# Interleaving the normalisation of a triangle product with output units that do not need it, in a two-layer kernel

## The chip, the core and the metric

One core of one Trainium2 chip runs the whole kernel. The engines named below are TensorE (PE; PEld is its weight load), VectorE (DVE), ScalarE (ACT), GpSimd (POOL) and the queue of SyncE (SP), which here only issues transfers. The metric is the device time of one execution in microseconds; the time of a kernel is the median of its runs.

## The reference, cut to what matters

The input x is 512 x 512 positions of 64 channels. Layer 0 normalises it by groups, then works on the normalised value `x`:

```python
xn = _ln(x, norm_w, norm_b)                       # over the 64 channels
left  = (xn @ left_w  + left_b)  * mask * sigmoid(xn @ lgate_w + lgate_b)
right = (xn @ right_w + right_b) * mask * sigmoid(xn @ rgate_w + rgate_b)
out_gate = sigmoid(xn @ ogate_w + ogate_b)
out = einsum('bkjd,bkid->bijd', left, right)      # the triangle product
out = (_ln(out, onorm_w, onorm_b) @ out_w + out_b) * out_gate
x1 = x + out
...
x2 = x1 + spectral(group_norm(x1))                # layer 1: 12 x 12 Fourier modes
```

The mask is 1 where both the row and the column of a position are set. At most 256 of the 512 rows are set in this case, so the product has to be formed for 256 x 256 positions only. A row that is not set has a product of zero: its `_ln(...) @ out_w + out_b` is the same 64 numbers for every column.

## The kernel before, in words

The function `compact` does the work. Rows are ranked so that the set rows come first. Four stages follow one another: (1) statistics of x for the group norm, (2) left and right for the set rows and columns, (3) the triangle product, written to DRAM as `tri_d` one channel at a time, (4) the stage that the change touches, followed by the last one, (5), which adds the inverse transform to x1 and writes the output.

Stage 4 has a hand-written order (`tc.manual_schedule()`): a loop over steps s (L1193) emits, for each step, one instruction group after another, and every engine runs its own instructions in that order. Eight steps (`SIZE`) make a unit. There are two kinds of unit.

* **Product units** (`first` = 8 of them, L920, the first 64 steps). A unit is 32 columns of the product. A step loads 512 positions of `tri_d` (`load_product`, L1022, on the SP queue, six steps ahead of use), multiplies them by a joint weight `both` = [centring matrix | output weight] (`centered`, L1048, matmul at L1058: eight matmuls over 64 rows each), squares one half of the result on ACT (L1078) and copies the other half to SBUF (L1079). Every two steps DVE sums the squares into `totals` (L1083). Once per unit ACT takes the square root (`root`, L1089) and DVE the reciprocal (L1263), into `factors`. DVE multiplies by the factors (L1271), POOL adds the bias row (L1278), and SP writes the result to `u_d` in DRAM.
* **Gate units** (32 of them, `units`, L922: column block `jc` of 16, `half` 0 for set rows and 1 for the others). A unit is 32 columns by 256 rows of x, gathered by POOL's indirect transfers (`load`, L1091). A step transposes 512 positions (`transpose`, L1030; PE at L1038, ACT's copy at L1040), multiplies them by `center_x` (`times`, L1045, tile c_ps) and, 12 steps later, by `gate_x` (tile w_ps). ACT squares c_ps (L1076), DVE sums (L1083), and root and reciprocal give `rs_n`. DVE multiplies w_ps by it (L1274) and adds the gate's bias (L1280), ACT takes the sigmoid (L1221), POOL multiplies by u (`gated`, L1109: a row of `u_d`, fetched by `load_u` at L1097, for half 0, the bias row for half 1) and adds to x (`added`, L1113). DVE takes the statistics of the sum for layer 1 (L1168, 32 instructions a unit), PE transforms it along the rows (`transform`, L1140), `save` (L1146) keeps the modes of both halves of one column block together, and SP stores x1.

`LEAD` = 13 steps lie between the transpose of a step and its multiplication by the factors. `scratch`, which holds totals, factors, the bias rows and sums of the statistics, lies in PSUM; x, u, z, the squares and the statistics lie in SBUF. The helper `rsqrt_steps` (L197 to L215) is an inverse square root of nine DVE instructions (L204 to L214); its tiles v, w, h and y lie in SBUF. Stage 2 uses it for its own norm, three instructions at a time from a list `todo`; stage 4 does not.

Of the kernel before, what the change touches and what calls it, by code (L numbers as in the profile page):

```python
# [17 lines left out]
P = 128  # L18
N = 512
# [27 lines left out]
def conv_preact_kernel(ctx: ExitStack, tc: tile.TileContext, t: dict):  # L47
# [149 lines left out]
    def rsqrt_steps(pool, total, scale, eps, shape, y=None):  # L197

        v, w, h, out = (pool.tile(shape, F32, name="rq_" + k) for k in ("v", "w", "h", "out"))
# [421 lines left out]
    def compact(fc):  # L621
# [4 lines left out]
        modes_d = dram.tile([N, M2, C], F32, name="modes_d")  # L626
# [204 lines left out]
        with tc.tile_pool(name="tri", bufs=1) as trp:  # L831
# [88 lines left out]
            first = K * 2 // 64  # L920

            units = [(jc, half) for jc in range(NJ) for half in ((1, 0) if jc < NJ - 1 else (0, 1))]  # L922
            total_g = (first + len(units)) * SIZE
            with tc.manual_schedule(), tc.tile_pool(name="late", bufs=1) as lp:
# [23 lines left out]
                def columns(h, pool):  # L948

                    q = P if h < 3 else P - JC  # L950
                    by = modes_t.rearrange("p (m k) c -> p m (k c)", k=2)
                    ps = pool.tile([P, 4, P], F32, name="t_ps").rearrange("p i k -> p (i k)")[:, : MODES * M2]
                    ps = ps.rearrange("p (m n) -> p m n", m=MODES)
                    for m in range(MODES):
                        nc.tensor.matmul(ps[:, m, :], by[:q, m, :], col_basis[:q, h, :], start=h < 3 or m == 0, stop=h < 3)
                    if h < 3:
                        nc.vector.tensor_add(sums, sums, ps)
                    return ps

                def fetch(h):  # L960

                    q = P if h < 3 else P - JC
                    (nc.scalar if h == 3 else nc.sync).dma_start(modes_t[:q], modes_d[h * P : h * P + q])
# [26 lines left out]
                with tc.tile_pool(name="np_x", bufs=LEAD + 2) as tp, tc.tile_pool(name="np_q", bufs=2) as sqp, tc.tile_pool(  # L990
                    name="np_s", bufs=3
                ) as small, tc.tile_pool(name="oz", bufs=4) as zp, tc.tile_pool(
                    name="o1", bufs=1
                ) as s1, tc.tile_pool(name="np_n", bufs=1, space=PSUM) as ps_n, tc.tile_pool(name="opf", bufs=1, space=PSUM) as ps_f, ExitStack() as products:
# [4 lines left out]
                    both = lp.tile([P, P], F32, name="both")  # L999
                    for h in range(2):  # L1000
                        hs = slice(h * C, (h + 1) * C)
                        nc.vector.tensor_copy(both[hs, :C], center[hs, hs])
                        nc.vector.tensor_copy(both[hs, C:], weights["out"][hs, hs])
# [15 lines left out]
                    def x_of(k):  # L1019
                        return place(order[k % RING])  # L1020
# [9 lines left out]
                    def transpose(s):  # L1030
                        k, n = divmod(s, SIZE)
                        if k < first:
                            return
                        flat = x_of(k - first).rearrange("p n c -> p (n c)")
# [4 lines left out]
                        xts[s] = tp.tile([P, 4, P], F32, name="xt_c")  # L1039
# [8 lines left out]
                    def centered(s):  # L1048
                        if s >= first * SIZE:
                            return times(ps_c, "c_ps", s, center_x)  # L1050

                        ps = ps_y.tile([P, 2, 4, P], F32, name="y_ps")
                        q, e = divmod(s, 2)
                        of = products_t[q % 4][:, e * N : (e + 1) * N].rearrange("p (i k) -> p i k", i=4)
                        for i in range(4):
                            for h in range(2):
                                hs = slice(h * C, (h + 1) * C)
                                nc.tensor.matmul(ps[:, h, i, :], of[hs, i, :], both[hs], start=True, stop=True)  # L1058
# [4 lines left out]
                    def raw(s):  # L1063
                        return xts[s].rearrange("p h (i c) -> p (h i) c", c=C).rearrange("p (h i) c -> p h i c", h=2)
# [5 lines left out]
                    def squared(s, cps):  # L1070
# [4 lines left out]
                        if s >= first * SIZE:  # L1075
                            nc.scalar.activation(sq, cps, AF.Square)  # L1076
                        else:
# [56 lines left out]
                    def transform(k, r):  # L1134
                        jc, half = units[k]
                        if k % 2 == 0 and r == 0:
                            fs[jc] = ps_f.tile([P, N], F32, name="f_ps")
                        for g in range(4):
                            o = r * JC + 8 * g
                            nc.tensor.matmul(  # L1140
                                fs[jc][32 * g : 32 * g + 32, :], hb[:, 2 * half + r, :],
                                x_of(k)[:, o : o + 8, :].rearrange("p j c -> p (j c)"),
                                start=(k % 2 == 0 and r == 0), stop=(k % 2 == 1 and r == 1), tile_position=(0, 32 * g),
                            )

                    def save(jc):  # L1146
                        ft = places[:, 7 * 64 * C + M2 * C : 7 * 64 * C + 32 * C].rearrange("p (j c) -> p j c", c=C)
                        nc.scalar.copy(ft.rearrange("p j c -> p (j c)"), fs.pop(jc))
                        if jc == NJ - 1:
                            ps = ends[0].rearrange("p m n -> p (m n)")  # L1150
                            for j in range(8):
                                for k in range(2):
                                    e = spread_e[:, j, k].rearrange("p m n -> p (m n)")
                                    nc.tensor.matmul(
                                        ps[k * C : (k + 1) * C], ft[:, j, :], e,
                                        start=False, stop=(j == 7), tile_position=(0, k * C),
                                    )
                            return
                        for g in range(4):
                            o = jc * JC + 8 * g  # L1160
                            queue = nc.scalar if jc == NJ - 2 else nc.sync
                            queue.dma_start(modes_d[o : o + 8].rearrange("j m c -> m j c"), ft[32 * g : 32 * g + M2])

                    def statistics(k, groups):
                        if k % 4 == 0 and 0 in groups:
                            st[k // 4] = s1.tile([P, G, 4, 6], F32, name="stats2c", bufs=2)
                        for g in groups:
                            nc.vector.bn_stats(st[k // 4][:, g, k % 4, :], x_of(k)[:, :, 2 * g : 2 * g + 2])  # L1168
# [23 lines left out]
                    loaded = 0  # L1192
                    for s in range(-LEAD, total_g + 2 * SIZE):  # L1193
                        k, n = divmod(s, SIZE)
                        v = k - first

                        def held(i):
                            return 0 <= v - i < len(units)

                        while loaded < K // 8 and 2 * loaded - LEAD - 5 <= s:  # L1200
                            load_product(loaded)
                            loaded += 1
# [3 lines left out]
                        if s + LEAD - 1 == first * SIZE:  # L1206
# [3 lines left out]
                        if 0 <= s < total_g:  # L1210
                            wps = raw(s) if k < first else times(ps_w, "w_ps", s, gate_x)
# [3 lines left out]
                        if n in (0, 4) and held(1):  # L1215
                            transform(v - 1, n // 4)

                        if n % 2 == 0:
                            i, c = (0, n // 2 - 1) if n >= 2 else (1, 3)
                            if held(i):  # L1220
                                nc.scalar.activation(zs[v - i, c], zs[v - i, c], AF.Sigmoid)  # L1221
                        if n == 5 and 0 <= k + 1 < first + len(units):
# [3 lines left out]
                        if n == 5 and held(1) and v % 2 == 0:  # L1226
                            save(units[v - 1][0])
                        if n == 3 and held(2) and v % 4 == 1:
                            join_squares(v // 4 - 1)

                        if n % 2 == 1:
                            i, c = (0, (n - 3) // 2) if n >= 3 else (1, 3)
# [301 lines left out]
```

## Time and profile before

| what | value |
|---|---|
| median of 3 runs (lowest to highest) | 1781.93 us (1778.47 to 1782.34) |
| the profiled execution's own time | 1777.78 us |
| its span, from the first to the last instruction | 1776.0 us |
| DVE busy, of the span | 1413.7 us (80%) |
| PE busy | 1567.8 us (88%) |
| POOL busy | 936.5 us (53%) |
| ACT busy | 933.0 us (53%) |
| first multiplication of a product unit (L1271) | at 643.98 us |
| first multiplication of a gate unit (L1274) | at 750.30 us |
| last bias add of a gate unit (L1280) | at 1446.62 us |

All times below are microseconds from the span's start. A view by windows gives, for each stretch, the busy time of every engine, the clock that was granted to TensorE and the mean busy share of the 16 DMA engines. A view by groups gives line, engine, operation, output and inputs, shapes and count; then busy time and the mean length of one instruction in ns; then the idle time of the engine just before them, and what ended it. A timeline lists instructions in order: start, length, engine, line, operation, and in brackets the idle time before it.

### The profile page before, as it was taken

The numbers are of one execution on the slowest core, as the hardware profiler recorded it, in microseconds if no ns is written. First come the engines' busy times: TensorE is split into PE (matmuls) and PEld (weight loads), VectorE is DVE, ScalarE is ACT, GpSimd is POOL, SyncE is SP. The second block draws the span as 40 slices with busy tenths as digits, with TensorE's granted clock in tenths as the row PEclk, the third lists the DMA queues.
The fourth block names the chain that finished last, engine by engine and source line by source line (L and its number), as shares of the span: only waits on it lengthen the run. The fifth ranks groups of instructions, "written<-read, shape, count | busy, mean of one in ns | idle before, by whom it ended". The sixth has DMA issues, their size and how long they took to land. (4 is left out here: it accounts for less than half of the span.)

```text
span 1776.0 us, 32619 instructions
## 1 busy us (share of the span) xinstructions
PE 1567.8 (88%) x10918; PEld 1242.0 (70%) x10918; DVE 1413.7 (80%) x2982; ACT 933.0 (53%) x1660; POOL 936.5 (53%) x695
## 2 busy tenths in 40 slices
PE   6779799997999978899999999999999977998772
PEld 5667666662899867787888888888888745665341
DVE  7989678887455568688999999999999984865451
ACT  3666566663333266676777777777777742011000
POOL 4666211111000037698999999999999881111110
PEclk9999999999899999899999999999999976555555
DMA  7999278878898789868767767776776699999999
GB/s 281 386 386 388 107 206 227 229 229 245 279 305 303 257 246 347 298 196 296 265 242 257 253 233 259 264 249 239 249 264 244 212 318 400 425 427 427 426 427 385
DMA packets 192593, 518.48 MB, mean 292 GB/s; under 512 B 37664, under 2 KB 104480, under 8 KB 151456
## 3 DMA queue, kind: packets, MB, share of 16 engines
q1 hardware_dynamic: 156112, 295.65, 47.5%
q0 software_dynamic: 32832, 218.45, 33.4%
q10 hardware_dynamic: 3472, 2.20, 0.5%
q8 instruction: 89, 1.46, 0.3%
q14 instruction: 88, 0.72, 0.1%
HBM read 311.60 MB, written 204.60 MB: 291 GB/s over the span
## 5 line engine op out<-in xcount | busy, mean ns | idle before, releaser
L1045 PE MATMUL w_ps<-gate_x,xt_c 128*128 128x128 f32 x2048 | 280.5, 281 | 30.0 <-DVE z_t L1274 28.6
L1113 POOL TENSOR_TENSOR places<-places,z_t 128x1024 f32<-128x1024 f32 x127 | 301.3, 2372 | 8.0
L1045 PEld LDWEIGHTS w_ps<-gate_x,xt_c 128*128 128x128 f32 x2048 | 252.0, 194 | 46.4 <-DVE z_t L1274 44.6
L1045 PE MATMUL c_ps<-center_x,xt_c 128*128 128x128 f32 x2048 | 277.0, 279 | 0.8 <-ACT xt_c L1040 0.4
L1045 PEld LDWEIGHTS c_ps<-center_x,xt_c 128*128 128x128 f32 x2048 | 252.8, 194 | 3.8 <-ACT xt_c L1040 3.0
L1440 PE MATMUL l_ps<-places,rinv 24*128 24x512 f32 x512 | 206.2, 1118 | 29.3 <-DVE places L1447 19.0
L1168 DVE BATCH_NORM_STATS2 stats2c<-places 128x6 f32<-128x128 f32 x1024 | 220.5, 278 | 9.9 <-POOL places L1113 9.9
L1083 DVE TENSOR_REDUCE scratch<-sq_c 128x16 f32<-128x1024 f32 x160 | 194.6, 1216 | 31.1 <-ACT sq_c L1078 16.1
L1221 ACT ACTIVATE z_t<-z_t 128x1024 f32<-128x1024 f32 x128 | 135.5, 1058 | 131.8 <-DVE z_t L1280 131.1
L1440 PEld LDWEIGHTS l_ps<-places,rinv 24*128 24x128 f32 x512 | 119.8, 302 | 110.8 <-DVE places L1447 56.9
L1278 POOL TENSOR_TENSOR z_t<-z_t,bias_row_out 128x1024 f32<-128x1024 f32 x32 | 75.6, 2363 | 226.3 <-PE y_ps L1058 202.1
L1040 ACT ACTIVATE xt_c<-t_ps,ab_xc 128x512 f32<-128x512 f32 x256 | 176.0, 688 | 11.5 <-PE t_ps L1038 10.6
L1274 DVE TENSOR_TENSOR z_t<-w_ps,rs_n 128x512 f32<-128x512 f32 x256 | 172.0, 672 | 6.2 <-PE w_ps L1045 6.1
L1076 ACT ACTIVATE sq_c<-c_ps 128x512 f32<-128x512 f32 x256 | 150.8, 589 | 31.4 <-PE c_ps L1045 30.8
L1280 DVE TENSOR_TENSOR z_t<-z_t,scratch 128x1024 f32<-128x1024 f32 x128 | 156.3, 1221 | 9.9 <-ACT rs_n L1089 3.7
L688 DVE BATCH_NORM_STATS2 stats1c<-x_ps 128x6 f32<-128x512 f32 x256 | 157.1, 682 | 7.7 <-PE x_ps L687 7.4
L1109 POOL TENSOR_TENSOR z_t<-z_t,places 128x1024 f32<-128x1024 f32 x64 | 151.8, 2371 | 14.6 <-ACT z_t L1221 14.4
L1038 PE MATMUL t_ps<-c_ident,places 128*128 128x128 f32 x1024 | 158.4, 278 | 0.0
L1038 PEld LDWEIGHTS t_ps<-c_ident,places 128*128 128x128 f32 x1024 | 118.5, 142 | 51.4 <-issue 51.4
L1447 DVE TENSOR_TENSOR places<-places,l_ps 128x512 f32<-128x512 f32 x176 | 109.3, 682 | 55.2 <-DMA places<-x_h,dst_i 42.1
L1109 POOL TENSOR_TENSOR z_t<-z_t,bias_row_out 128x1024 f32<-128x1024 f32 x63 | 149.4, 2372 | 5.8 <-ACT z_t L1221 5.5
L673 ACT COPY xc<-xg 128x128 f32 x352 | 105.0, 298 | 66.1 <-POOL xc L673 47.1
(214 smaller groups left out, 2557.0 us busy)
## 6 DMA issues: line engine op xcount, KB each, us to landing
x_h<-places SPq DMA_DIRECT2D x64, 1024.0 KB
out_x<-places SPq DMA_DIRECT2D x44, 1024.0 KB
places<-u_d SPq DMA_DIRECT2D x512, 64.0 KB
out_x<-lx_t SPq DMA_DIRECT2D x20, 1024.0 KB
rbc<-rs_d POOLq DMA_DIRECT2D x32, 512.0 KB, 7.1
left_d<-o_c SPq DMA_DIRECT2D x64, 256.0 KB
right_d<-o_c SPq DMA_DIRECT2D x64, 256.0 KB
left_raw<-left_d SPq DMA_DIRECT2D x64, 256.0 KB
```

Of the source, the lines that this page charges most:

```text
L688: nc.vector.bn_stats(stats[:, 0, 16 * (jc % quarter) + 4 * r + c, :], ps.rearrange("p i k -> p (i k)"))
L1038: nc.tensor.transpose(tps[:, i, :], flat[:, o : o + P], ident)
L1040: nc.scalar.activation(xts[s], tps, AF.Identity, bias=ab1[:, 2:3])
L1045: nc.tensor.matmul(ps[:, 2 * i : 2 * i + 2, :], xts[s][:, i, :], w, start=True, stop=True)
L1076: nc.scalar.activation(sq, cps, AF.Square)
L1083: nc.vector.tensor_reduce(totals[k % 2][:, 8 * (n - 1) : 8 * (n + 1)], sqs.pop(s // 2), AX.X, ALU.add)
L1109: nc.gpsimd.tensor_mul(zs[k, c], zs[k, c], u)
L1113: nc.gpsimd.tensor_add(xr, xr, zs.pop((k, c)))
L1168: nc.vector.bn_stats(st[k // 4][:, g, k % 4, :], x_of(k)[:, :, 2 * g : 2 * g + 2])
L1274: nc.vector.tensor_mul(z[:, 8 * odd : 8 * odd + 8, :], wps, rs)
L1280: nc.vector.tensor_add(z, z, bias_ps["ogate"].unsqueeze(1).to_broadcast([P, 16, C]))
L1440: nc.tensor.matmul(ps.rearrange("p j o -> p (j o)"), rinv[h, b, :], it[h], start=True, stop=True, tile_position=(32 * g, 0),)
```

## The change

The 40 units stay, and so do their sizes. Their order and, for the first 16, their instructions change.

* The first 16 units (`MIXED`) alternate: a gate unit of the rows that are not set (half 1), a product unit, and so on: eight of each. Then come the other 24 gate units, two of half 0 after each of half 1.
* In those 16 units the gate unit takes the joint matmul too: weight [center_x | gate_x] over 64 rows, one half squared by ACT, the other copied to SBUF by ACT; the c_ps and w_ps matmuls of these units are gone, and DVE multiplies the SBUF copy by factors in PSUM.
* In those 16 units the factors come from `rsqrt_steps` on DVE (nine instructions of 128x64 per unit, three in each of the last three steps of the unit before) and no longer from ACT's root and DVE's reciprocal. The 24 gate units that follow keep root and reciprocal.
* The two halves of a column block are now far apart, so each has its own `modes_d`, its own save (30 saves with transfers, not 15) and its own column transforms (8 in all, not 4).
* Everything that was keyed to "unit v" is now planned by step in `agenda`. For the mixed gate units stores, transform, save and statistics come four steps later than before relative to the unit, and loads 29 steps ahead, not 21. There are eight z tiles in the mixed phase (four of them in a free part of `places`), four after it.

```diff
-    def rsqrt_steps(pool, total, scale, eps, shape, y=None):
+    def rsqrt_steps(pool, total, scale, eps, shape, y=None, out=None):
...
-        v, w, h, out = (pool.tile(shape, F32, name="rq_" + k) for k in ("v", "w", "h", "out"))
+        v, w, h = (pool.tile(shape, F32, name="rq_" + k) for k in ("v", "w", "h"))
+        if out is None:
+            out = pool.tile(shape, F32, name="rq_out")
...
-        modes_d = dram.tile([N, M2, C], F32, name="modes_d")
+        modes_d = [dram.tile([N, M2, C], F32, name=f"modes_d{h}") for h in range(2)]
...
-            first = K * 2 // 64
+            MIXED = K * 2 // 32
-            units = [(jc, half) for jc in range(NJ) for half in ((1, 0) if jc < NJ - 1 else (0, 1))]
+            units = [one for i in range(MIXED // 2) for one in ((i, 1), None)]
+            for i in range(NJ // 2 - 1):
+                units += [(NJ // 2 + i, 1), (2 * i, 0), (2 * i + 1, 0)]
+            units += [(NJ - 2, 0), (NJ - 1, 0), (NJ - 1, 1)]
...
                     def centered(s):
-                        if s >= first * SIZE:
+                        if s >= MIXED * SIZE:
                             return times(ps_c, "c_ps", s, center_x)
                         ps = ps_y.tile([P, 2, 4, P], F32, name="y_ps")
-                        q, e = divmod(s, 2)
-                        of = products_t[q % 4][:, e * N : (e + 1) * N].rearrange("p (i k) -> p i k", i=4)
+                        of, w = xts.get(s), both[0]
+                        if of is None:
+                            of, w = products_t[s // 2 % 4][:, s % 2 * N : (s % 2 + 1) * N], both[1]
+                            of = of.rearrange("p (i k) -> p i k", i=4)
...
+                        elif units[s // SIZE] is not None:
+                            by_half = lambda t: t.rearrange("p (i h) c -> p h i c", h=2)
+                            nc.scalar.activation(by_half(sq), cps[:, :, :, :C], AF.Square)
+                            nc.scalar.copy(by_half(raw(s)), cps[:, :, :, C:])
...
+                        if n == 5 and 0 <= k + 1 < MIXED:
+                            todo += rsqrt_steps(
+                                rq, totals[(k + 1) % 2], 1.0 / C, EPS, [P, SIZE * 8], out=factors[(k + 1) % 2]
+                            )[1]
+                        for step in todo[:3]:
+                            step()
+                        del todo[:3]
                         if n == 7 and k + 1 in rss:
-                            nc.vector.reciprocal(factors[(k + 1) % 2] if k + 1 < first else rss[k + 1], rss[k + 1])
+                            nc.vector.reciprocal(rss[k + 1], rss[k + 1])
...
+                                rs = factors[k % 2] if k < MIXED else rss[k]
+                                rs = rs[:, 8 * n : 8 * n + 8].unsqueeze(2).to_broadcast([P, 8, C])
                                 nc.vector.tensor_mul(z[:, 8 * odd : 8 * odd + 8, :], wps, rs)
```

## The prediction, as it was put on record

> **What bounds the kernel now.** I began with the chain of waits: from 1469 us on it is stage 5, whose output transfers keep the DMA engines at a share of 1.00 and more. The change does not touch that stage, so whatever stage 4 gains or loses moves the end by as much. Next came windows over stage 4 (busy us of PE, PEld, DVE, ACT, POOL with their counts; clock; DMA share; GB/s).
>
> ```profile
> core 0: us, PE busy (x) PEld busy (x) DVE busy (x) ACT busy (x) POOL busy (x), PEclk, DMA share, GB/s
> 644.00:716.00 72.00, 56.82 (x746) 49.24 (x742) 63.76 (x78) 49.80 (x101) 56.51 (x26) 1.00 0.98 322
> 716.00:735.00 19.00, 15.21 (x109) 13.47 (x110) 8.32 (x10) 8.59 (x17) 8.77 (x5) 0.64 0.80 298
> 750.00:778.00 28.00, 28.00 (x254) 26.56 (x252) 20.89 (x28) 22.61 (x33) 23.77 (x12) 1.00 0.67 216
> 1000.00:1300.00 300.00, 292.22 (x2476) 258.77 (x2475) 294.37 (x693) 224.22 (x330) 286.07 (x139) 0.99 0.72 251
> ```
>
> In the gate units (last row) DVE is busy 294.4 of 300 us. It waits for nobody there, and POOL is close behind. In the product units (first row) DVE is also the fullest engine, 63.8 of 72, while the DMA engines are full. At the end of that phase a load of the product came late: DVE idles 10.7 of 19 us in the second row. So DVE's work sets the pace in both phases; what a mixture can win is only DVE's idle time at their seams.
>
> ```profile
> L1113 POOL TENSOR_TENSOR places<-places,z_t 128x1024 f32<-128x1024 f32 x127 | 301.3, 2372 | 8.0
> L1168 DVE BATCH_NORM_STATS2 stats2c<-places 128x6 f32<-128x128 f32 x1024 | 220.5, 278 | 9.9 <-POOL places L1113 9.9
> L1083 DVE TENSOR_REDUCE scratch<-sq_c 128x16 f32<-128x1024 f32 x160 | 194.6, 1216 | 31.1 <-ACT sq_c L1078 16.1
> L1274 DVE TENSOR_TENSOR z_t<-w_ps,rs_n 128x512 f32<-128x512 f32 x256 | 172.0, 672 | 6.2 <-PE w_ps L1045 6.1
> L1280 DVE TENSOR_TENSOR z_t<-z_t,scratch 128x1024 f32<-128x1024 f32 x128 | 156.3, 1221 | 9.9 <-ACT rs_n L1089 3.7
> ```
>
> The groups show what DVE reads: every large instruction has at most one input in SBUF; its partner (w_ps, scratch) is in PSUM. POOL's instructions last 2.37 us, eight per gate unit.
>
> **The change part by part, DVE's own work.** The window 1000 to 1300 holds 111 multiplications of L1274, eight per unit: 300 / 13.9 = 21.6 us per gate unit. Its reciprocal (0.54) goes: 21.05 left. A product unit takes 72.0 / 6 = 12.0; its reciprocal (0.56) and DVE's wait for ACT's root (3.0 us over the six) go: 10.95 left. The multiplication from the SBUF copy costs the same (L1271 0.684 against L1274 0.672). What comes is nine small instructions per unit. Stage 2 runs the same ones at half the width, the groups first, then the timeline:
>
> ```profile
> L207 DVE TENSOR_TENSOR rq_w<-rq_y,rq_v 128x32 f32<-128x32 f32 x16 | 3.1, 192 | 0.6
> ```
> ```profile
> 210.98 0.18 DVE L205 TENSOR_SCALAR rq_y<-rq_v 128x32 int32<-128x32 int32 x1
> 211.19 0.19 DVE L207 TENSOR_TENSOR rq_w<-rq_y,rq_v 128x32 f32<-128x32 f32 x1
> ```
>
> They start 0.21 to 0.23 apart. The 128x128 instructions of L230 and L241 start 0.36 apart, so 64 columns should cost about 0.25 (bounds 0.20 and 0.28). A pair of units costs 21.05 + 10.95 + 18 x 0.25 = 36.5; eight pairs 292. Before, the product phase took 750.3 - 644.0 = 106.3 with its late load, and eight gate units 172.8: 279. **Term 1: +13** (bounds +6 and +17).
>
> **Start.** Before, PE waited 6.6 us for tri_d and the first multiplication came 19.4 us after the first y_ps. Now unit 0 is a gate unit, whose x was gathered while POOL idled (202 us before its first L1278). It begins at 618.5: eight steps at about 1.75 (PE 0.60 + 1.07; ACT 0.57 + 0.50 + 0.58), five of about 1.2, and 2.3 of small instructions: 641 instead of 644. **Term 2: -3** (-6 to +4).
>
> **Seam.** The 7.1 us that DVE idles from 750 to 778 have to do with the first gate unit (3.2 of them a wait for POOL's first sums); the seam now falls in a running pipeline, but still swaps the PSUM pools, and the first u rows have 9 steps to arrive, not 11. **Term 3: -3** (-8 to +3).
>
> **What costs nothing or little.** PE loses half of the matmuls' row time in eight units; it waits for DVE anyway. Four more column transforms cost DVE four adds of 0.455: **term 4, +2**; their matmuls and the 15 more saves (ACT 0.59 each, four SP issues each) lie beside DVE's work: ACT, without its table loads in the mixed phase, needs some 28 of 36 us a pair. POOL needs eight sums of 2.37, four bias adds of 2.36 and two issues of 0.98: 30.4 of 36.5; it stays second. SP: product loads stand behind u_d writes that wait for POOL; six steps of 2.3 us ahead are 14 us, a lag of two steps leaves them early. If that cover went, PE would stall as in 716 to 735.
>
> **Term 5: the new wait.** Eight of the nine small instructions read SBUF through both inputs or go from SBUF to SBUF, and in this phase POOL is working. The trace before has this meeting only in stage 1, where L230 reads set_mean and stats1c, both in SBUF, beside POOL's short copies:
>
> ```profile
> 62.59 0.30 POOL L673 COPY xc<-xg 128x128 f32 x1
> 62.90 0.32 DVE L230 SCALAR_TENSOR_TENSOR stats1c<-set_mean,stats1c 128x128 f32<-128x128 f32 x1
> 62.95 0.43 POOL L673 COPY xc<-xg 128x128 f32 x1
> ```
>
> The copy that starts just after the DVE instruction takes 0.43 instead of 0.30 us (again 0.45 at 195.06): the later one waits. Where L241 starts with 0.12 us of a copy left, it is not visibly longer. So the wait of a DVE instruction that comes second is between zero and a POOL instruction, 2.37 us. For POOL's long sums I take the mirror image of the row: who comes second waits until the other is done.
>
> The Trainium skill speaks against this change here. Its page "SBUF — State Buffer", section "Who interferes with whom", says that a Vector instruction with two SBUF inputs contends with a GpSimd instruction that reads SBUF, that the first holds the shared port for its whole length, and that the other blocks. By that rule alone the sum is the one of the walk that follows; by the undelayed L241 rows it is terms 1 to 4. No run shown here has a long GpSimd instruction beside such a DVE instruction.
>
> A walk through one pair, DVE from 0, steps 0 to 7 gate, 8 to 15 product; a step is 0.78 for four statistics, 1.2 for a reduction at even steps, 0.7 per multiplication and 1.15 per bias add; the sigmoid ends 1.6 after the add. z0 is ready at 5.35, z1 at 10.7; POOL starts at 7.0: gated, load, added, gated. Step 5: the second small instruction meets a POOL sum until 15.2 (wait 0.8), POOL's next one slips in before the third (2.4). Step 6: 2.0, then 2.35; then POOL has no z left and step 7 is free. Gate unit: 7.55. Step 13: 1.5 and 2.35; step 14: 1.15; after that POOL is dry: 5.0. Pair: 36.2 + 12.55 = 48.7. Unit 0's factors come before POOL works; of the other 15 bursts eight lie in gate units and seven in product units: 8 x 7.55 + 7 x 5.0 = **+95**. Ends: 0, and 12 POOL instructions a pair, 28.4 x 8 = 227, which the walk excludes because POOL runs dry.
>
> **Sum.** Against the profiled execution (1777.8, span 1776.0; the median of the runs is 4.1 higher, which I leave in the range): +13 - 3 - 3 + 2 + 95 = +104, **1882**. I take the full wait since the two stretched copies lost 0.13 and 0.15 us, about what the DVE instruction's reading takes (96 more columns, from 32 to 128, move its spacing from 0.22 to 0.36): they lost it whole, not shared.
>
> **Rivals.** (a) Only the first of a burst waits, DVE's next small instructions being ahead of POOL's next sum: 8 x 2.8 + 7 x 2.65 = 41: 1777.8 + 9 + 41 = 1828. For it: DVE's instructions follow each other within 0.25. Against: POOL's next sum starts 0.05 before the last one is recorded as ended. (b) No wait at all: 1787 (terms 1 to 4), high end 1804. For it: the L241 rows. (c) **Faster**: as (b), and the small instructions start 0.20 apart, while unit 0's gate work covers the start and the mixture covers the late loads of 716 to 735: +6 - 6 - 8 + 2 = -6: 1772. It decides as soon as DVE's mean wait per small instruction of the 120 is under 0.05 us. For it: DMA 0.98 and DVE idle in 716 to 735; against: DVE has no other idle time to give.
>
> **How the numbers follow.** Full wait 1850 to 1905: 0.46. (a) 1804 to 1850: 0.17. Beyond 1905: 0.07. No wait: 0.30, of which 0.15 faster, 0.06 the same, 0.09 slower. About 0.2% is what a measurement of this kernel can tell from no change; slower by more: 0.46 + 0.17 + 0.07 + 0.09 = 0.79. The range 1772 to 1905 leaves out the 0.07 above and half of (c). The likeliest case's own range is 1850 to 1905.
>
> **What would show it.** Right: the rq rows of stage 4 at mean lengths over 1 us or with gaps before them, DVE's pair at 45 to 50 us, POOL less full than 30 in 36. (a): 41 to 43 us a pair. Wrong: rq rows of 0.2 us with no gap beside 2.37 us POOL rows, pairs of 36 to 37 us. Term 2: first multiplication at 641. If pairs are near 32 us, my price of the nine instructions was wrong.

## The result, and the profile after

The kernel takes 1907.74 us (median of 4 runs, 1904.42 to 1920.06), the one before 1781.01 beside it: a ratio of 1.0726, 95% interval 1.0677 to 1.0775. The change costs 7.3%. The profiled execution has a span of 1906.8 us. The forecast of 1882 had the sign and the mechanism, but 1907.7 lies just beyond the upper end of its range, 1905. So the question is where some 26 us more came from.

The windows of the kernel after, cut at the first multiplication of a mixed unit, the first of the other gate units and the last bias addition (columns as in the prediction: DVE is the third busy time, POOL the fifth):

```profile
654.40:1024.00 369.60, 253.16 (x2373) 207.48 (x2374) 348.20 (x598) 208.71 (x356) 244.29 (x116) 0.78 0.56 184
1024.00:1580.80 556.80, 514.90 (x4212) 453.31 (x4212) 506.12 (x1187) 387.65 (x581) 486.25 (x233) 0.95 0.77 257
```

In the first row DVE is full: 348 of 370 us. In the second, the 24 ordinary gate units, whose own instructions the change leaves as they were (their order, their saves and the fetches of columns it does not), DVE is busy in only 506 of 557 us, 91%, where it had 294.4 of 300, 98%, before. Cut in the same way, the forecast and the measurement are:

| stretch | forecast | measured | difference |
|---|---|---|---|
| first multiplication of stage 4 at | 641 | 654.4 | +13.4 |
| mixed phase (106.3 + 172.8 + 13 + 95) | 387.1 | 369.6 | -17.5 |
| 24 gate units (697.5 - 172.8 - 3 + 2) | 523.7 | 556.8 | +33.1 |
| behind them | 328.2 | 326.0 | -2.2 |
| span | 1880.0 | 1906.8 | +26.8 |

The predicted wait is there, and it is smaller than forecast; two other stretches took more. First the wait. The small instructions in the view by groups of the kernel after, from 654 to 1024 us:

```profile
L210 DVE TENSOR_TENSOR rq_h<-rq_w,rq_y 128x64 f32<-128x64 f32 x15 | 26.3, 1751 | 0.0
L207 DVE TENSOR_SCALAR rq_y<-rq_v 128x64 int32<-128x64 int32 x15 | 24.4, 1625 | 0.5
L209 DVE TENSOR_TENSOR rq_w<-rq_y,rq_v 128x64 f32<-128x64 f32 x15 | 20.9, 1391 | 0.5
L211 DVE SCALAR_TENSOR_TENSOR rq_h<-rq_h 128x64 f32<-128x64 f32 x15 | 18.6, 1242 | 0.5
L214 DVE TENSOR_TENSOR rq_w<-rq_y,rq_v 128x64 f32<-128x64 f32 x15 | 3.2, 213 | 0.0
```

L209 and L214 do the same thing on the same tiles, and one takes 1391 ns, the other 213. The idle time ahead of them is nil: a wait for POOL shows as a longer instruction, not as a gap. Four rows of 15 instructions at 0.22 would be 13.2 us; they are 90.2, so DVE waits 77 us. The timeline of one burst shows for what (only POOL's and the small instructions are copied):

```profile
757.86 2.34 POOL L1141 TENSOR_TENSOR places<-places,z_t 128x1024 f32<-128x1024 f32 x1
757.88 2.41 DVE L209 TENSOR_TENSOR rq_w<-rq_y,rq_v 128x64 f32<-128x64 f32 x1
...
765.75 2.36 POOL L1141 TENSOR_TENSOR places<-places,z_t 128x1024 f32<-128x1024 f32 x1
765.79 2.40 DVE L211 SCALAR_TENSOR_TENSOR rq_h<-rq_h 128x64 f32<-128x64 f32 x1
```

POOL's addition begins 0.02 to 0.04 us ahead of the small instruction, and that one ends less than 0.1 us after it: here who comes second waits for the whole of the first. L214 to L216, a step later, meet no POOL instruction, since POOL has no z left.

Next the 24 gate units. What DVE waits for there, from 1024 to 1581 us (total, times, longest):

```profile
DVE sums L969 <- PE t_ps L965: 22.0, 2, 11.1
DVE z_t L1355 <- PE w_ps L1065: 12.4, 9, 6.2
DVE stats2c L1203 <- POOL places L1141: 7.1, 2, 6.9
```

The first row, 22.0 us in two waits, is an addition that the prediction priced at 0.455 us. It stands behind PE's column transform, and that behind a fetch. The timeline of SP's queue and DVE around the first of the two:

```profile
1056.70 20.53 SPq L1128 DMA_DIRECT2D places<-u_d  x32
1077.82 3.76 SPq L1197 DMA_DIRECT2D modes_d<-places  x4
1081.62 0.42 SPq L975 DMA_DIRECT2D places<-modes_d  x1
1093.95 0.46 DVE L969 TENSOR_TENSOR sums<-sums,t_ps 128x288 f32<-128x288 f32 x1 [11.06 <-PE t_ps L965]
```

SP issues a load of u, 32 transfers in 20.5 us, then the four of a save, and only then the fetch; PE's column transform starts at 1088.63 us, after 8.35 us of waiting for it. SP's queue as a whole has far less slack there: before, from 750 to 1448 us, it stood 220.0 us waiting for POOL's sums (places, L1113), after, from 1024 to 1581 us, 22.3 (L1141). Last, the start. In the kernel after, the first gather of x on POOL, and behind it stage 3's first transposition on PE:

```profile
442.75 1.03 POOL L640 DMA_INDIRECT places<-in_x,src_i  x1 [22.31 <-PE row_out L821]
453.01 1.08 PE L875 MATMUL side_ps<-c_ident,left_raw 128*128 128x128 f32 x4 [9.51 <-DMA left_raw<-left_d]
```

PE waits 9.5 us for stage 3's first input; before it was 4.3. The first product comes at 463.2 us; before it came at 453.4. Four gathers of 1 MB each now stand ahead of those loads.

### The profile page after: what moved, and what is told of

Read it like the earlier page. It is cut to its first block, busy times and chain, and to the rows that moved or that the text cites. A ratio compares the mean times of both kernels' runs of the same rounds, so it can differ in the third digit from the quotient of the medians.

```text
span 1906.8 us, 33003 instructions
## 1 busy us (share of the span) xinstructions
PE 1590.1 (83%) x11014; PEld 1243.3 (65%) x11014; DVE 1516.2 (80%) x3118; ACT 953.0 (50%) x1707; POOL 935.9 (49%) x695
## 3 DMA queue, kind: packets, MB, share of 16 engines
q0 software_dynamic: 32832, 218.45, 31.4%
## 5 line engine op out<-in xcount | busy, mean ns | idle before, releaser
L1137 POOL TENSOR_TENSOR z_t<-z_t,bias_row_out 128x1024 f32<-128x1024 f32 x63 | 149.2, 2368 | 319.2 <-ACT z_t L1282 318.9
L1141 POOL TENSOR_TENSOR places<-places,z_t 128x1024 f32<-128x1024 f32 x127 | 300.8, 2369 | 7.5
L1065 PE MATMUL w_ps<-gate_x,xt_c 128*128 128x128 f32 x1536 | 212.6, 283 | 17.0 <-DVE z_t L1355 16.4
L1065 PE MATMUL c_ps<-center_x,xt_c 128*128 128x128 f32 x1536 | 210.6, 281 | 12.4 <-ACT xt_c L1060 12.2
L1065 PEld LDWEIGHTS w_ps<-gate_x,xt_c 128*128 128x128 f32 x1536 | 191.9, 196 | 30.0 <-DVE z_t L1355 28.3
L1065 PEld LDWEIGHTS c_ps<-center_x,xt_c 128*128 128x128 f32 x1536 | 192.6, 197 | 14.8 <-ACT xt_c L1060 13.4
L1058 PE MATMUL t_ps<-c_ident,places 128*128 128x128 f32 x1024 | 173.6, 296 | 3.3 <-ACT xt_y L1060 2.5
L1137 POOL TENSOR_TENSOR z_t<-z_t,places 128x1024 f32<-128x1024 f32 x64 | 151.7, 2370 | 32.1 <-ACT z_t L1282 19.9
L1060 ACT ACTIVATE xt_c<-t_ps,ab_xc 128x512 f32<-128x512 f32 x192 | 132.2, 688 | 48.1 <-PE t_ps L1058 35.2
L1080 PE MATMUL y_ps<-both_x,xt_y 64*128 64x128 f32 x1024 | 98.9, 353 | 68.4 <-ACT xt_y L1060 68.3
L1080 PEld LDWEIGHTS y_ps<-both_x,xt_y 64*128 64x128 f32 x1024 | 86.1, 252 | 82.1 <-ACT xt_y L1060 76.0
L1355 DVE TENSOR_TENSOR z_t<-w_ps,rs_n 128x512 f32<-128x512 f32 x192 | 129.2, 673 | 12.6 <-PE w_ps L1065 12.4
```

Of the source, the lines that this page charges most:

```text
L1058: nc.tensor.transpose(tps[:, i, :], flat[:, o : o + P], ident)
L1060: nc.scalar.activation(xts[s], tps, AF.Identity, bias=ab1[:, 2:3])
L1065: nc.tensor.matmul(ps[:, 2 * i : 2 * i + 2, :], xts[s][:, i, :], w, start=True, stop=True)
L1080: nc.tensor.matmul(ps[:, h, i, :], of[hs, i, :], w[hs], start=True, stop=True)
L1137: nc.gpsimd.tensor_mul(zs[k, c], zs[k, c], u)
L1141: nc.gpsimd.tensor_add(xr, xr, zs.pop((k, c)))
```

## The experiments

**Theory:** DVE's small instructions wait for POOL because of what they do in SBUF; the loads of u crowd SP's queue in the 24 gate units; the early gathers delay stage 3. **Rivals:** PE at its lower clock (0.78 in the mixed phase) paces that phase; the mixture itself, not the nine instructions, costs the time; the late fetches have another cause. Each ratio below is to the kernel before, run beside it.

### The wait behind POOL

`y_in_psum`: one operand of each small instruction is moved to PSUM. The fifth reads rq_h twice, so rq_h is written twice, to SBUF and (`again`) to PSUM, and the fifth reads one of each.

```diff
+        def twice():
+            vec.tensor_mul(h, w, y)
+            if again is not None:
+                vec.tensor_mul(again, w, y)
...
-            lambda: vec.tensor_mul(h, w, y),
-            lambda: vec.scalar_tensor_tensor(h, h, -10.0 / 3.0, h, ALU.add, ALU.mult),
+            twice,
+            lambda: vec.scalar_tensor_tensor(h, h if again is None else again, -10.0 / 3.0, h, ALU.add, ALU.mult),
...
-                                rq, totals[(k + 1) % 2], 1.0 / C, EPS, [P, SIZE * 8], out=factors[(k + 1) % 2]
+                                rq, totals[(k + 1) % 2], 1.0 / C, EPS, [P, SIZE * 8], y=scratch[:, 3, C:],
+                                out=factors[(k + 1) % 2], again=scratch[:, 2, :C],
```

> All of the change stands; in the mixed phase rq_y lies in PSUM, and rq_h is written a second time there (one more instruction per unit), so that no small instruction has both its inputs in SBUF. Theory (the small instructions wait for POOL because of their second SBUF input): the rq rows fall from 107 us in the mixed phase to about 150 x 0.23 = 35, the phase from 370 to some 300, the time from 1907 to about 1836. Rival (the mixed phase is paced by PE at its lower clock of 0.78, or by the half rows of its matmuls, and the waits only fill time that is lost anyway): the rq rows become short, idle time before the reductions takes their place, and the time stays above 1890.

Measured: 1849.63 us, ratio 1.0389 (1.0366 to 1.0413), so 58 us less than the kernel after. Groups of this kernel:

```profile
L213 DVE TENSOR_SCALAR scratch<-rq_v 128x64 int32<-128x64 int32 x16 | 3.6, 228 | 0.5
L215 DVE TENSOR_TENSOR rq_w<-scratch,rq_v 128x64 f32<-128x64 f32 x16 | 3.6, 224 | 0.6
L217 DVE SCALAR_TENSOR_TENSOR rq_h<-scratch,rq_h 128x64 f32<-128x64 f32 x16 | 3.6, 224 | 0.5
```

All ten rows are at 0.21 to 0.23 us although POOL works as before. The mixed phase falls from 369.6 to 306.0 us, and PE's clock in it is 0.87, so PE's 0.78 was a consequence. The first rival falls. Not all of the 77 us come back, but 63.6: 3.5 are the added instruction, DVE's waits for ACT's squares and root in that phase rise from 11.3 to 17.2, and some 4 us stay unexplained.

Which of the instructions wait? `one_left` does not write rq_h twice (only the fifth has both inputs in SBUF); `seed_twice` is y_in_psum plus a second copy of the TENSOR_SCALAR, from SBUF to SBUF, with one input.

```diff
# one_left, against y_in_psum
-                                out=factors[(k + 1) % 2], again=scratch[:, 2, :C],
+                                out=factors[(k + 1) % 2],
# seed_twice, against y_in_psum
+                vec.tensor_scalar(idle.bitcast(I32), v.bitcast(I32), -0.5, float(0x5F3759DF), ALU.mult, ALU.add)
```

> rq_y lies in PSUM as in y_in_psum, but rq_h is not written twice: of the nine small instructions only the fifth (rq_h from rq_h and rq_h, both in SBUF) has two inputs in SBUF. Theory A (each such instruction pays for itself, a rest of one POOL instruction): its mean is 1.0 to 1.4 us, the others 0.22, 16 x 1.0 = 16 us more than y_in_psum's 1850 less 3.5 for the instruction that is not doubled: 1862. Theory B (a burst waits until POOL has no work left, however few instructions wait, as pool_halved makes likely): its mean is 3 to 5 us, 1900.

> y_in_psum with one instruction more per unit: the second small instruction, a TENSOR_SCALAR with one input, also writes a copy to SBUF that nobody reads. It is the only one of the eleven that goes from SBUF to SBUF. Theory (such an instruction waits for POOL although it has one input): its mean is 1.5 us or more, as L207's 1.6 in the kernel after, the rest 0.22; 1850 + 16 x 1.5 = 1874. Rival (only two inputs in SBUF make a wait, and L207 waited for something else): mean 0.22, 1853.

Measured: 1857.83 (ratio 1.0446, 1.0421 to 1.0470) and 1863.21 (1.0465, 1.0446 to 1.0484). The waiting row and a neighbour, one_left first, then seed_twice:

```profile
L217 DVE SCALAR_TENSOR_TENSOR rq_h<-rq_h 128x64 f32<-128x64 f32 x15 | 25.5, 1703 | 0.5
L218 DVE SCALAR_TENSOR_TENSOR scratch<-rq_h,scratch 128x64 f32<-128x64 f32 x15 | 3.4, 229 | 0.5
```
```profile
L215 DVE TENSOR_SCALAR rq_idle<-rq_v 128x64 int32<-128x64 int32 x15 | 29.2, 1946 | 0.0
L212 DVE TENSOR_SCALAR scratch<-rq_v 128x64 int32<-128x64 int32 x15 | 3.4, 228 | 0.5
```

In each kernel exactly the one expected row is long. Both kinds wait: two inputs in SBUF, and one input with both ends in SBUF; the same operation to PSUM takes 228 ns. For one_left theory A comes close in time (1862 expected), while its row, 1703 ns, is longer than the 1.0 to 1.4 us of A and far from the 3 to 5 of B. seed_twice pays 14 us, not 24: its row holds 26 us of waiting, but DVE's waits for ACT fall from 17.2 to 9.6 beside it, and the mixed phase grows by 18 (324.1 against 306.0). In one_left it is the same: 22 us of waiting, less 3.5 and less 5.9, leave 12.6, close to the 12.9 by which its phase (318.9) is longer.

The Trainium skill, page "SBUF — State Buffer", section "Who interferes with whom", names both kinds: two SBUF inputs beside a GpSimd instruction that reads SBUF, and tensor_scalar, which can enter a two-port mode. These two kernels agree with it: 1703 and 1946 ns for the two rows, 228 and 229 for their neighbours.

`pool_halved`: POOL's products and sums of the mixed phase, and the product's bias additions, are cut into two of 128x512 (shown for the first).

```diff
-                        nc.gpsimd.tensor_mul(zs[k, c], zs[k, c], u)
+                        for a in (0, 8) if k < MIXED else ():
+                            nc.gpsimd.tensor_mul(zs[k, c][:, a : a + 8], zs[k, c][:, a : a + 8], u[:, a : a + 8])
```

> POOL's sums and products of the mixed phase are cut into two instructions of 128x512 each, about 1.2 us instead of 2.37. Theory (a small instruction waits until the one POOL instruction ahead of it has ended, whatever its length): the mean of the four long rq rows falls from 1.5 us to about 0.8, the waits from 77 us to some 40, the time to about 1872. Rival (the two engines share the bandwidth and POOL's amount of work decides): the rows stay at 1.5 us, 1905 or more.

Measured: 1916.54, ratio 1.0751 (1.0717 to 1.0784). Nothing is won; the nine rows together hold 107 us, as in the kernel after. The time is the rival's, but its mechanism, a shared bandwidth, does not explain why some rows became shorter and one longer (below). The timeline, DVE's instruction and POOL's from its view by engine:

```profile
665.29 6.13 DVE L207 TENSOR_SCALAR rq_y<-rq_v 128x64 int32<-128x64 int32 x1
```
```profile
664.00 2.49 POOL L1146 TENSOR_TENSOR places<-places,z_t 128x512 f32<-128x512 f32 x2
666.45 2.48 POOL L1138 TENSOR_TENSOR z_t<-z_t,bias_row_out 128x512 f32<-128x512 f32 x2
668.90 2.47 POOL L1146 TENSOR_TENSOR places<-places,z_t 128x512 f32<-128x512 f32 x2
```

These are six pieces of 1.2 us. L207 comes at about the start of the second and ends at 671.42, when the sixth has ended and POOL goes on to a gather. The instructions with two inputs do wait less (L209 from 1391 to 692 ns, L210 from 1751 to 1232), but L207 waits more (from 1625 to 2427), and L212 and L214 now meet a piece too. So "a rest of one POOL instruction" is not the rule: the TENSOR_SCALAR waited through five pieces. Nor is it alone in this. In the same kernel one L210 waited through four pieces that follow each other without a gap (from 901.65 to 906.59 us), and another through three:

```profile
901.80 4.89 DVE L210 TENSOR_TENSOR rq_h<-rq_w,rq_y 128x64 f32<-128x64 f32 x1
967.68 3.72 DVE L210 TENSOR_TENSOR rq_h<-rq_w,rq_y 128x64 f32<-128x64 f32 x1
```

In the kernel after, too, an L207 took 3.75 us and an L210 2.98, both more than one POOL instruction. When POOL's next piece goes ahead of the waiting instruction and when it does not, these runs do not show.

### One part alone

`root_back` keeps the mixture and takes ACT's root and DVE's reciprocal again; `factors_alone` is the kernel before with only the nine instructions in its product phase.

```diff
# root_back
-                        if n == 5 and MIXED <= k + 1 < len(units):
+                        if n == 5 and 0 <= k + 1 < len(units):
                             root(k + 1)
...
-                            nc.vector.reciprocal(rss[k + 1], rss[k + 1])
+                            nc.vector.reciprocal(factors[(k + 1) % 2] if k + 1 < MIXED else rss[k + 1], rss[k + 1])
# factors_alone: the kernel before, with
+                        if n == 5 and 0 <= k + 1 < first:
+                            todo += rsqrt_steps(rq, totals[(k + 1) % 2], 1.0 / C, EPS, [P, SIZE * 8], out=factors[(k + 1) % 2])[1]
```

> One part undone: in the mixed phase ACT takes the root and DVE the reciprocal into PSUM again, two instructions of 0.55 us a pair instead of eighteen of 0.25 and their waits. Theory (waits of 77 us and 3.4 us of DVE's own work a pair, 27 in all): 1907 - 104 = 1803, less what ACT's four table loads a pair (5.1 us on an engine with some 29 of 34) give back, so 1800 to 1815. Rival (ACT becomes the bound, its root standing behind sigmoids that wait): pairs of 38 us and more, 1840.

> The kernel before with one part of the change alone: the factors of the eight product units by the nine small instructions of DVE, no mixture. Theory (waits behind POOL's sums, 5.1 us a burst as in the kernel after, 77 / 15): a product unit takes 12.0 - 0.56 - 0.5 + 2.25 + 5.1 = 18.3, 50 us more in eight, of which the late load of 716 to 735 us (10.7) is covered: 1781 + 40 = 1820. Rival (POOL's products and sums of gate units make the waits; its bias additions alone are 9.5 of 12 us and leave gaps): 1 us a unit, 1785 to 1790.

Measured: root_back 1862.82, ratio 1.0472 (1.0433 to 1.0511); factors_alone 1787.82, ratio 1.0048 (1.0033 to 1.0062). Both theories missed, and the rivals came closer. In root_back the pair takes 323.1 / 8 = 40.4 us: DVE waits 31.4 us for ACT's root and 27.8 for its squares, so a wait for ACT takes the place of the wait for POOL. In factors_alone L210 waits 1 us, and the others hardly at all (L207 354 ns, L209 226): POOL has only the bias additions and idles between them. So neither part alone explains the 7.3%. The nine instructions are cheap beside a POOL with gaps, and the mixture without them still costs 82 us, 44 of them in the mixed phase (323.1 against 279); together they put DVE's small instructions beside POOL's backlog of a gate unit.

### The 24 gate units

Four kernels on the fetches of columns: `columns_later` adds the columns of two blocks a unit later; `saves_by_act` issues all saves and fetches from ACT; `fetch_ahead` and `fetch_ahead2` issue the fetches five steps earlier on SP, ahead of the load of u.

```diff
# columns_later
-                        at += SIZE
+                        at += 2 * SIZE if (half, h) in ((1, 1), (1, 2)) else SIZE
# saves_by_act
-                            queue = nc.scalar if (jc, half) == (NJ - 2, 0) else nc.sync
-                            queue.dma_start(modes_d[half]...
+                            nc.scalar.dma_start(modes_d[half]...
# fetch_ahead (in fetch_ahead2 the block (1, 3) keeps its step)
-                        plan(at, "fetch", half, h)
+                        plan(at - 5, "fetch", half, h)
```

> The column transforms of blocks (1,1) and (1,2) come two units after their fetch, not one. Theory (the fetch stands on SP's queue behind a load of u with 32 issues of 0.64 us, and PE waits for it with everything that is queued behind it): the two waits of 11 us of DVE for the addition of the column sums go, 1907 - 22 = 1885. Rival (the fetch is late because its data, the saved rows, are late, and the wait moves elsewhere): at most -5, 1902 or more.

> All saves of modes and all fetches of columns are issued by ACT instead of SP, nothing else. Theory (SP's queue holds them: a load of u takes it 18 to 25 us, and two such loads fall on three gate units of 65 us): fetches are issued at their step, land within 10 us, and the waits of DVE for the column sums (two of 11 us) and the wait for the last saves (6 to 7 us, twice) go: 1907 - 22 - 10 = 1875. Rival (SP's loads of u are the pace themselves): the time that the columns gave back goes into POOL's waits for places<-u_d, and the time stays above 1898.

> The seven fetches of columns on SP are issued five steps earlier, ahead of the load of u behind which they stood (step 1 of a unit instead of 6; loads of u come at step 3); the additions keep their place. Theory (order on SP's queue): the two waits of 11 us for the column sums go, 24 gate units take 535 instead of 557 us, 1907 - 22 = 1885. Rival (the fetches' data or the loads of u are late themselves): the wait moves to the next fetch or to POOL's products, as in columns_later: 1900 or more.

> As fetch_ahead, but the last fetch on SP keeps its old step. (In fetch_ahead that fetch came ahead of the additions of the block before it, which then used the wrong block and waited 18 us for it.) Theory (order on SP's queue): no wait over 3 us for the column sums is left, 24 gate units take about 535 us, 1885. Rival: a wait for another late transfer takes the 18 us, 1900 or more.

Measured: 1903.72 (ratio 1.0697, 1.0673 to 1.0721), 1944.45 (1.0902, 1.0865 to 1.0938), 1903.71 (1.0696, 1.0677 to 1.0715) and 1901.85 (1.0679, 1.0653 to 1.0706). None gives the 22 us. Each removes the two waits at their places, and the time goes elsewhere. In columns_later the next fetch, at 1217 us, comes 10 us too late. In saves_by_act DVE's wait for the column sums is 2.3 us, but ACT stands 45 us behind its own issues of the saves (14 times), and its squares come late. fetch_ahead made a wait of 18 us itself, since its last fetch goes ahead of the additions of the block before. The waits of DVE in the gate units of fetch_ahead2, to be read against 22.0, 12.4 and 7.1 above:

```profile
DVE stats2c L1203 <- POOL places L1141: 17.0, 10, 6.3
DVE sums L969 <- PE t_ps L965: 10.9, 2, 8.0
DVE z_t L1355 <- PE w_ps L1065: 9.2, 10, 3.0
```

The sum is 37 instead of 42. So the order of the fetch is not the whole cause, but one place where it shows. `u_half` leaves out every second transfer of a load of u; `u_thin` issues all 32 and moves half the bytes.

```diff
# u_half
+                            if j % 2 == 1:
+                                continue
                             nc.sync.dma_start(us[jc][:, j], u_d[:, bass.ds(slot, 1)].rearrange("p o r c -> p (o r) c"))
# u_thin
+                            nc.sync.dma_start(us[jc][:, j, 0:1], u_d[:, bass.ds(slot, 1), 0, :])
```

> The kernel after with every second one of the 32 transfers of each load of u left out (half of u stays what lay there, so the output is not the reference's). Theory (SP's issues of the loads of u, 20 us each and two to every three gate units, make the fetches, the last saves and u itself late): SP needs 10 us a load, the waits of DVE in the gate units (22 for the column sums, 12 for w_ps, 7 for POOL) fall below 8 in all, 24 units take 525 instead of 557, 1875. Rival (DVE's waits there do not come from the loads of u): 555, 1905.

> All 32 transfers of each load of u are issued, but each moves only the first of its two rows, 32 KB instead of 64 (the other half of u stays what lay there, so the output is not the reference's). If the number of issues on SP is what counts: 1903 to 1907, gate units 550 to 557. If the bytes and the DMA engines' time count: as u_half, 525 and 1875.

Measured: 1872.38 (ratio 1.0514, 1.0486 to 1.0542) and 1900.63 (1.0687, 1.0639 to 1.0736). The gate units take 521.2 us in u_half and 548.2 in u_thin, against 556.8. DVE's largest waits in u_half's:

```profile
DVE z_t L1357 <- PE w_ps L1065: 3.9, 7, 1.4
DVE stats2c L1205 <- POOL places L1143: 2.4, 1, 2.4
```

The wait for the column sums is gone without a change to fetch or addition. u_half halves both issues and bytes and gives 35.6 us; u_thin halves the bytes alone and gives 8.6, no more than columns_later (548.5 us), which leaves the loads whole. The DMA engines' mean share falls from 0.77 to 0.71 in both, while SP's time for a load falls only in u_half (8.5 to 10.2 us, against 17.7 to 22.2 in u_thin): it is mostly SP's time. Before, 16 loads of u lay in 32 gate units, one in two (19 of 43 us of SP); now two lie in three (some 40 of 65), beside twice as many saves. Per gate unit SP's loads of u take 13.2 us where they took 9.6, and its saves 2.4 where they took 0.8; no run spaces the loads as before, so how much each of the two costs is not shown.

### The start, and sums of edits

`gathers_held` puts a copy on POOL that waits for stage 3's fourth channel ahead of the gathers; `gathers_held2` makes that copy write into the gathers' buffers; `no_gathers` leaves the four gathers out.

```diff
# gathers_held
+                    if c == 3:
+                        nc.gpsimd.tensor_copy(held, out_t[:, 1, :1])
# gathers_held2
+                        first = places[:, : 4 * JC * C].rearrange("p (a b) -> p a b", a=4)
+                        nc.gpsimd.tensor_copy(first[:, :, 0], out_t[:, 1, :4])
# no_gathers
+                        if nth[k] < 2:
+                            nc.gpsimd.memset(x_of(k)[:, r * JC : (r + 1) * JC].rearrange("p j c -> p (j c)"), 1.0)
+                            return
```

> POOL's first four gathers of x, 1 MB each, wait for the fourth channel of stage 3 (a copy of one column on POOL stands ahead of them). Theory (they collide with the first loads of stage 3): stage 3's first product comes at 454 instead of 463 us, as in the kernel before, and the end comes 8 us earlier, 1899. Rival (4 MB cost the DMA engines their time wherever they lie, stage 3 being at a DMA share of 0.90): the delay moves into stage 3, and the time stays at 1905 or more.

> As gathers_held, but the copy on POOL writes one column into each of the four buffers that the gathers fill, so that the gathers must follow it (in gathers_held they went ahead of it at 444 us). Theory (collision with stage 3's first loads): first product of stage 3 at 454 us instead of 463, first multiplication of stage 4 about 8 us earlier, 1899. Rival (the 4 MB cost stage 3 their time wherever they lie): stage 3 starts at 454 but ends at 628 all the same, 1905 to 1909.

> The first four gathers of x (units 0 and 2) are left out, POOL fills their buffers with ones instead, so the output of those two units is not that of the reference. Theory (4 MB of gathers cost stage 3 their time, wherever they lie): first product of stage 3 at 454 us, first multiplication of stage 4 about 646 instead of 654, 8 to 9 us less: 1899. Rival (the later start has to do with stage 4's new first unit alone): first multiplication at 653 or later, 1906.

Measured: 1914.58 (ratio 1.0761, 1.0717 to 1.0805), 1917.29 (1.0733, 1.0701 to 1.0765) and 1899.43 (1.0682, 1.0664 to 1.0701). gathers_held tells nothing: without a shared tile the gathers went ahead of the copy, at 444 us as before. In gathers_held2 they came at 473 us, and PE was busy 22.2 of the 30 us from 470 to 500 where it had been 30.0: the loss only moved. Without the gathers (POOL fills the buffers itself) stage 3's first product comes at 455.6 us instead of 463.2, and stage 4's first multiplication at 645.0 instead of 654.4. So 4 MB beside stage 3 cost it some 8 to 9 us, at both of the places tried.

`all_three` joins y_in_psum, saves_by_act and gathers_held2; `y_psum_fetch` joins y_in_psum with fetch_ahead (so it too uses one block for the last two additions), `y_psum_fetch2` with fetch_ahead2.

> y_in_psum, saves_by_act and gathers_held2 together. If the three causes are all there is beside DVE's own work: mixed phase 306 us as in y_in_psum, first multiplication at 644, 24 gate units of 21.7 us and the additions of the columns 525, 326 behind them: 1801. Rival (a further bound, the DMA engines or PE's clock, takes what the three give back): 1830 or more.

> y_in_psum and fetch_ahead together. Theory (two separate causes): 1850 less what fetch_ahead gains alone; 1828 if that is 22. Rival (with POOL's waits gone SP has less time, so the fetches come late all the same): 1845.

> y_in_psum and fetch_ahead2 together. Two separate causes: 1850 - 22 = 1828. If SP and the DMA engines have too little time once POOL's waits are gone: 1845.

Measured: 1888.61 (ratio 1.0578, 1.0544 to 1.0612), 1848.67 (1.0382, 1.0358 to 1.0405) and 1844.63 (1.0356, 1.0329 to 1.0382). all_three carries the two edits that lost time: its gate units take 585.2 us. y_psum_fetch2 has the lowest time of the kernels with the mixture that compute everything, still 3.6% above the one before; its gate units take 554.5 us. No version here beats the kernel before.

## Why the prediction missed its range

1. **What bounds the kernel, and the sign**: right. DVE sets the pace in the mixed phase, and most of what is added to it is paid (y_in_psum shortens DVE's busy time in that phase by 71.0 us, from 348.2 to 277.2, and the phase by 63.6).
2. **Term 1, DVE's own work (292 us)**: right. 369.6 us less the 77 of waiting is 292.6. That is a subtraction; the run without these waits, y_in_psum, takes 306.0, or 302.5 less its added instruction, with 5.9 us more of waiting for ACT.
3. **Term 5, the wait of a second comer**: right in mechanism and place (steps 5 and 6 long, step 7 free, POOL dry between), 18 us too dear: 77 instead of 95, or 5.1 us for each of 15 bursts instead of 6.3. Most of the 18 lies in the product units: the walk gave each burst there 5.0 us, with a whole POOL instruction (2.35) for the third small one, and the timelines show 3.1 and no wait for the third (L209 at 0.23), since POOL was itself waiting for DVE's next z then; in the gate units it is 6.9 instead of 7.55. The rows were to be over 1 us (four of the nine are, 1.2 to 1.8), the pair 45 to 50 us (46.2), POOL less full than 30 in 36 (244 of 370). That one instruction can wait longer than one POOL instruction was not foreseen.
4. **Term 2, the start (-3)**: wrong, +10.4 (654.4 against 644.0). The prediction counted the early gathers as free because POOL idles there, and did not ask whose DMA time they take; no_gathers gives back 9.4 us. Stage 4 began at 628.05 instead of 618.5, 9.5 late; most of the rest of the 13.4 is in unit 0, whose first two steps took 3.05 us each on PE (y_ps at 632.05, 635.10 and 638.16), not 1.75.
5. **Term 4 and "what costs nothing or little"**: this is the step that failed, and the largest error. It gave the column transforms +2 and laid the saves "beside DVE's work"; it looked at SP's queue for the product loads of the mixed phase alone. What the runs showed in its place: the new order of units packs the loads of u closer, two in three units, beside twice as many saves, and the fetches, saves and products of u then come late on SP's queue: +33.1 us in units whose work on DVE is nearly what it was (21.1 us busy a unit, 20.9 before). u_half, with half the issues, takes 35.6 us back.
6. **Term 3, the seam (-3)**: too small to be told apart.

Two errors of +13.4 and +33.1 and two of -17.5 and -2.2 make the 26.8 us. That the time lies so near the range is luck: without the 17.5 us by which the mixed phase came out cheaper, it would lie some 20 us beyond. The prediction shows no working for the upper end of 1905; the upper bounds of terms 1 to 3 (4, 7 and 6 us above their values) and the 4.1 us of the median make 1903. A bound for SP's queue in the 24 gate units was missing.

## What to carry to other kernels

A small instruction on DVE can cost as much as what POOL is doing at that moment: look where its operands lie, and put one of them (with a single input, the output) into PSUM if POOL works on SBUF beside it. When the order of units changes, count the issues on each in-order queue for every stretch of the new order, those of untouched code included. A load that is issued in an engine's idle time can still delay the stage it lands in.

## What the runs showed of the hardware

* A TENSOR_SCALAR from SBUF to SBUF with one input waits for POOL (1946 ns against 228 with its output in PSUM); POOL's instructions were not lengthened by it (in the kernel after, 2362 to 2368 ns in the mixed phase, 2370 to 2371 for the same additions and products behind it).
* Such an instruction waited through five POOL pieces in a row (6.13 us), and a TENSOR_TENSOR through four (4.89 us); cutting POOL's instructions in half left the nine rows at 107 us together.
* Issuing a load of u, 32 transfers of 64 KB whose addresses come from registers, takes SP 17.6 to 22.5 us in the kernel after, and 17.7 to 22.2 with 32 KB each (u_thin): the number counts more than the bytes.
